# Dealing a top-p search out differently between TensorE's steps: first attention of a four-layer graph network

## The chip, the cores and the metric

The kernel runs on one core of a Trainium2 chip. The metric is the device time of one execution in microseconds (us), lower is better. Three executions of the kernel before took 3474.58, 3479.55 and 3481.09 us; their median is 3479.55 us.

## What is computed

There are 3327 nodes with 256 features each, and a dense adjacency of 3327 x 3327. Four layers follow one another, each of the form `x = layernorm(x + layer(x, adj))`. The change lies in layer 3:

```python
def _top_p_attention(X, W1, W2, W3):
    q = X @ W1.T @ W2.T
    k = X @ W3.T
    probs = softmax(q @ k.T / TAU, axis=-1)
    # keep the largest entries of each row until their sum reaches 0.9
    A = probs * mask
    return A / maximum(A.sum(-1, keepdims=True), 1e-12)

R = S + eye(N);  R = R / R.sum(-1, keepdims=True)
for n in range(2):
    A = _top_p_attention(Xa, W1, W2, W3)
    Xf = R @ Xf
    Xa = A @ Xa
    Z = Z + Xf @ U1[n].T + Xa @ U2[n].T
return layernorm(X + Z)
```

Here `S` is the adjacency. The loop over `n` runs twice; the change touches the first round only, "the first attention". For each row it needs scores against all nodes, a search for the value down to which entries are kept, the product of the kept entries with `X` (values), and the product of the adjacency's rows with `X` (the spread).

## The kernel before

Rows are worked in 26 tiles of 128, in 13 pairs (`nh`). A pair's two products, spread and values, are each made with a scheme that multiplies 2 x 2 blocks with seven products instead of eight. One step of such a product handles one of 13 column blocks with `products`: seven products, which the trace shows as fourteen matmul records. Before its products a spread step may need sums of adjacency blocks (`cb`, VectorE, in `part` of `diffused_pair`, one for two steps), and a value step needs sums of transposed weights (`sw`, VectorE, in `mix` of `attended_pair`). When 13 steps are done, `assembled` puts the seven partial results together into `c` with eight VectorE operations, which read the accumulator in PSUM. For the spread, `with_own` then adds each node's own part into `F`.

For the values, TensorE first transposes the weights: `turn` writes four transposed blocks into `tp` (two buffers), ScalarE copies them to `wt`, and VectorE mixes them to `sw` (three buffers). `attended_pair` makes three turns and two mixes when it is first advanced; after that each value step makes a turn three blocks ahead, a mix two blocks ahead and its products.

Scores of a tile (`scores`) come in four groups: each is two or more matmuls into the only `sc` buffer and a ScalarE copy into `e`. The search for a tile (`search_short`) is a generator in slices, and a call of `look` runs one slice of the search at the head of a queue: five slices of MAX8 over 26 segments (5, 5, 5, 5 and 6 of them), six rounds on the candidates (the first also starts ScalarE's exponential over the whole row), a crossing, which needs a short exponential on ScalarE and finds the smallest kept value, two slices that mask half a row each, and an end. `finish` runs what is left of the queue.

After the values of a pair, `first` projects each of its tiles in three more steps: transposes of the spread and value results into `tp` and a copy `xt`, a projection with a VectorE sum `s`, and the second projection with keys and queries for the next attention. Its beginning scales the values by a normalizer on ScalarE.

A pass of the main loop, for pair i, has two halves. The first half runs seven spread steps of pair i+1 (`stage`), four score groups of tile 2i+2, the projection of the preceding pair's even tile, and at step 5 `attend_to(i)`, which finishes the queue and starts the values of pair i. Then come value steps 0 to 6. The second half runs spread steps 7 to 12, the four score groups of tile 2i+3 and the projection of the odd tile, and then value steps 7 to 12. Between all these stand the looks. Ahead of the loop, tile 1's spread (`diffused_first`) and the scores of tiles 0 and 1 are made; behind it, the last two tiles.

The order on TensorE and VectorE is written out by hand in this stage: the wrappers `tensor` and `vector` keep every instruction of these two engines in program order (the trace puts them all on line 891, inside the wrapper, so they are told apart by their tiles). Instructions of ScalarE, GpSimd and the DMA queue on SP are put in order by the framework's planner. [...]

Of the kernel before, what the change touches and what calls it, by code (L numbers as in the profile page):

```python
# [50 lines left out]
def gnn_kernel(ctx: ExitStack, tc: tile.TileContext, n: int, a: dict, out: bass.AP):  # L51
# [3 lines left out]
    nh = nt // 2  # L55
# [121 lines left out]
    with tc.tile_pool(name="l1b", bufs=1) as wpool, tc.tile_pool(name="l1at", bufs=2) as l1at:  # L177
# [3 lines left out]
        with tc.tile_pool(name="l0", bufs=1) as pool, tc.tile_pool(name="l0w", bufs=2) as work, \  # L181
# [11 lines left out]
            for j0 in range(0, nh, J0):  # L193
                m = min(J0, nh - j0)
# [10 lines left out]
                y = slice(j0, j0 + m)  # L205
# [6 lines left out]
            for i in range(nh):  # L212
                p1, p2, p3, p4, p5, p6, p7 = halved(atp, cmb, psum, i, top, low, ts)
                c = work.tile([P, 2, D + 1], F32, name="c", bufs=1)
# [10 lines left out]
                for r in range(2):  # L225
                    it = 2 * i + r
# [3 lines left out]
                    y = work.tile([P, 2, HD], F32, name="y")  # L230
# [9 lines left out]
        with tc.tile_pool(name="l1aw", bufs=1) as cwork, tc.tile_pool(name="l1c", bufs=2) as ch, \  # L240
# [51 lines left out]
            for k, v in enumerate(("attn_src", "attn_dst")):  # L292
                r = scratch()[:, 0, :D]
# [17 lines left out]
            ends = []  # L311
# [219 lines left out]
            class Head:  # L531
# [70 lines left out]
                def finish(self):  # L602

                    c, w, e1 = self.c, self.w, self.e1
                    vec.tensor_sub(e1, e1, self.e)
                    vec.scalar_tensor_tensor(e1, self.v, 0.0, e1, op0=ALU.max, op1=ALU.add)
                    du = ch.tile([P, NG, WC], F32, name="du", bufs=1)[:, :, :w]
                    vec.tensor_mul(du, e1, us[c])
                    xs[c] = e1, du
# [103 lines left out]
            first = Head(0)  # L713
# [26 lines left out]
            turned = []  # L740
            for k, (c, s) in enumerate(states):
                w = us[c].shape[2]
                m = tiles_of(c)
# [59 lines left out]
                if c and 9 <= s < 9 + tiles_of(c - 1):  # L803
                    rs, nb = plus[:2]
                    i = s - 9
                    x = X[:, starts[c - 1] // P + i, :]
# [7 lines left out]
                if after:  # L814
                    if s == min(p["project"]):
                        pump(ends[c + 1] // P)
                    first = [lambda g=g: ahead.project(g) for g in p["project"].get(s, ())]
# [26 lines left out]
            m = tiles_of(nch - 1)  # L844
# [5 lines left out]
            for i in range(m):  # L850
                it = starts[nch - 1] // P + i
# [16 lines left out]
    with tc.tile_pool(name="l3", bufs=1) as pool, tc.tile_pool(name="l3d", bufs=1, space=DRAM) as dram:  # L868
# [135 lines left out]
        with tc.tile_pool(name="l2c", bufs=1) as cpool:  # L1004
# [5 lines left out]
            with tc.tile_pool(name="l2a", bufs=1) as wpool, \  # L1010
# [5 lines left out]
                r = cpool.tile([P, npad], F32, name="r")  # L1016
# [22 lines left out]
                m = wpool.tile([P, 2], F32, name="m")  # L1039
# [9 lines left out]
                f = wpool.tile([1, 1], F32, name="f")  # L1049
# [84 lines left out]
        tots, vs, kepts = ([pool.tile([P, nt], F32, name=f"{x}{p}") for p in range(2)] for x in ("tot", "v", "kept"))  # L1134
# [75 lines left out]
        def diffused_first(quads, psum, it, out):  # L1210

            own_part(it)
            acc = psum.tile([P, 2, 512], F32, name="acc")[:, 0, :D]
            for j0 in range(0, nt, 4 * JQ):
                m = min(4 * JQ, nt - j0)
                at = quads.tile([P, 5, JQ, P], F32, name="at", bufs=3).rearrange("p k j r -> p (k j) r")
                nc.sync.dma_start(at[:, :m, :], a["adjT"][it][:, j0:j0 + m, :])
                for j in range(m):
                    tensor.matmul(acc, at[:, j, :], X[:, j0 + j, :], start=(j0 + j == 0), stop=(j0 + j == nt - 1))
                yield  # L1220
            with_own(acc, it, out)

        def diffused_pair(quads, psum, i, b, out):
# [319 lines left out]
        def normalizer(sm, kept, total):  # L1543

            f = t1(sm, "f")
            vector.scalar_tensor_tensor(f, total, 1e-12, kept, op0=ALU.mult, op1=ALU.max)
            vector.reciprocal(f, f)
            return f
# [89 lines left out]
        with tc.tile_pool(name="l3w", bufs=2) as work, tc.tile_pool(name="l3s", bufs=4) as sm:  # L1638
# [13 lines left out]
            with tc.tile_pool(name="l3p", bufs=2, space=PSUM) as psum, tc.tile_pool(name="l3a", bufs=1) as quads:  # L1652
                fixed = True
                es, searches, xfs, todo, queue = {}, {}, [xf0], [], []
                flat = G.rearrange("p t d -> p (t d)")
                b = blocks(X, [flat[:, k * nh * HD:(k + 1) * nh * HD].rearrange("p (t d) -> p t d", t=nh) for k in range(4)])

                def look():
                    while queue and next(queue[0], queue) is queue:
                        queue.pop(0)  # L1660

                def finish():
                    while queue:
                        look()

                def logits(t):
                    return start(0, t, es, searches, search_short) if t < nt else iter(())

                def spreading(i):
                    x = diffused_pair(quads, psum, i, b, xfs) if i < nh else iter(())  # L1670
                    next(x, None)
                    return x

                def stage(spread, steps, groups, ends, then=lambda: None):
                    for k in range(steps):
                        next(spread, None)
                        if k % 2 == 0:
                            next(groups, None)
                        if k in (2, 3, 4):
                            next(ends, None)  # L1680
                        if k == 5:
                            then()
                        look()
                    for _ in groups:
                        pass
                    for _ in ends:
                        pass

                def attend_to(i):
                    turned[0] = attended_pair(quads, psum, (es[2 * i], es[2 * i + 1]), b)  # L1690
                    finish()
                    next(turned[0])

                turned = [None]
                for _ in logits(0):
                    pass
                queue.append(searches[0])
                spread = spreading(1)
                groups = logits(1)
                for _ in diffused_first(quads, psum, 1, xfs):  # L1700
                    next(groups, None)
                    for _ in range(3):
                        look()
                for _ in groups:
                    pass
                finish()
                queue.append(searches[1])
                for _ in range(7):
                    look()
                for i in range(nh - 1):  # L1710
                    ends = todo or [iter(()), iter(())]
                    stage(spread, 7, logits(2 * i + 2), ends[0], lambda: attend_to(i))
                    values = turned[0]
                    queue.append(searches[2 * i + 2])
                    for _ in range(7):
                        next(values)
                        look()
                    stage(spread, 6, logits(2 * i + 3), ends[1])
                    for _ in spread:
                        pass  # L1720
                    finish()
                    queue.append(searches[2 * i + 3])
                    for k in range(6):
                        if k == 3:
                            spread = spreading(i + 2)
                        next(values)
                        look()
                        if k % 3 == 2:
                            look()
                    c = next(values)  # L1730
                    todo = []
                    for r in range(2):
                        it = 2 * i + r
                        f = normalizer(sm, kepts[0][:, it:it + 1], tots[0][:, it:it + 1])
                        todo.append(first(quads, psum, it, c[:, r, :], f, xfs[it], "tp", c[:, r, :]))
                        next(todo[r])
                values = attended(quads, psum, es[nt - 2], X, acc=psum.tile([P, 2, 512], F32, name="acc")[:, 0, :D])
                next(values)
                ends = (x for y in todo for x in y)
                for it in (nt - 2, nt - 1):  # L1740
                    for _ in range(7):
                        acc = next(values)
                        if it == nt - 2:
                            look()
                            look()
                        next(ends, None)
                    acc = next(values)
                    if it == nt - 2:
                        finish()
                        values = attended(quads, psum, es[nt - 1], X, acc=psum.tile([P, 2, 512], F32, name="acc")[:, 0, :D])  # L1750
                        next(values)
                    f = normalizer(sm, kepts[0][:, it:it + 1], tots[0][:, it:it + 1])
                    c = quads.tile([P, 2, D], F32, name="c", bufs=1)[:, 0, :] if it == nt - 2 else quads.tile([P, 4, P], F32, name="sw", bufs=3)[:, :2, :].rearrange("p a b -> p (a b)")
                    for _ in ends:
                        pass
                    ends = first(quads, psum, it, acc, f, xfs[it], "tp", c)
                    next(ends)
                both(ends)
                fl0 = unresolved(sm, psum, 0)
                fixed = False  # L1760
# [210 lines left out]
```

## Time and profile before

The profile shows one execution. Times are in us.

| what | value |
|---|---|
| median of three executions | 3479.55 |
| the profiled execution, its own time | 3479.06 |
| its span, first to last instruction | 3477.3 |
| TensorE matmul busy | 3155.6 (91%) |
| VectorE busy | 2743.7 (79%) |
| ScalarE busy | 1738.5 (50%) |
| first attention, about | 1697 to 2617 |
| distance from pass to pass in it | 69.05 |
| mean granted TensorE clock, whole span | 0.966 |

"Busy" adds up the time in which an engine has an instruction under way. TensorE overlaps its matmuls, and their ends are modelled, so the distance from one start to the next says more than a duration. In timelines a row merges instructions of one kind that follow each other: start, time to the end of the last, engine, line, operation, output<-inputs, shape, count, and in brackets the idle time before and what ended it. `acc<-X,at`, `acc<-G,at` and `acc<-G,cb` are spread steps, `acc<-X,wt`, `acc<-G,sw`, `acc<-X,sw` and `acc<-G,wt` value steps, `tp<-ident,e` turns, `sc<-kT,q` scores, `tp<-U,xt` projections.

### The profile page before, as it was taken

Reading aid. Unit: us, or ns where it says so; the run is one execution under the profiler, and the core shown is the slowest. Engines: PE = TensorE matmul, PEld = TensorE weight load, DVE = VectorE, ACT = ScalarE, POOL = GpSimd, SP = SyncE. Lnnn points to the kernel's source line nnn. Section 1 sums busy time; section 2 is a strip of 40 time slices with the busy share of each in tenths; the row PEclk is TensorE's granted clock in tenths of the full one; section 3 lists DMA queues with packets and bytes.
Section 4 is the critical chain, followed back from the end, with each engine's and each line's share of the span. In section 5 each row is a group of like instructions: output and inputs, shape, how many; then the busy total and the mean of one; then the engine's idle time right before and its main releaser. Section 6 shows DMA issues by size and latency. Waiting matters only on the chain. (4 is left out here: it accounts for less than half of the span.)

```text
span 3477.3 us, 50356 instructions
## 1 busy us (share of the span) xinstructions
PE 3155.6 (91%) x18301; PEld 2570.0 (74%) x18301; DVE 2743.7 (79%) x6359; ACT 1738.5 (50%) x2764; POOL 938.9 (27%) x942
## 2 busy tenths in 40 slices
PE   8999888898987777999899999999998999999996
PEld 5998757676665555888678888888885777777775
DVE  4665368999999997777577777777755999999996
ACT  1000456766767774111233333333336888888883
POOL 0000245666656652111400000000002333333332
PEclk9999999999999988999999999999998999999998
DMA  6775334434343222444322322222213122222220
GB/s 198 253 246 183 114 90 127 109 106 121 101 114 87 68 60 97 147 143 153 97 74 62 88 66 80 63 87 67 79 40 105 56 63 70 62 68 66 66 66 16
DMA packets 206266, 344.32 MB, mean 99 GB/s; under 512 B 22223, under 2 KB 129167, under 8 KB 205871
## 3 DMA queue, kind: packets, MB, share of 16 engines
q1 hardware_dynamic: 205998, 340.92, 32.4%
q8 instruction: 148, 2.42, 0.3%
q14 instruction: 120, 0.98, 0.1%
HBM read 304.65 MB, written 36.21 MB: 98 GB/s over the span
## 5 line engine op out<-in xcount | busy, mean ns | idle before, releaser
L330 POOL TENSOR_TENSOR h<-du,row 128x2048 f32<-128x2048 f32 (+1 forms) x110 | 465.6, 4233 | 343.0 <-DVE hc L330 254.6
L330 DVE TENSOR_TENSOR_SCAN h<-dA,carry,h 128x512 f32<-128x512 f32 (+1 forms) x384 | 448.8, 1220 | 16.6 <-ACT dA L337 16.5
L337 ACT ACTIVATE dA<-t,A_log 128x512 f32<-128x512 f32 (+1 forms) x448 | 292.6, 658 | 147.2 <-DVE h L330 145.6
L1295 PE MATMUL acc<-F,at 128*128 128x256 f32 x1352 | 353.1, 387 | 0.0
L1340 PE MATMUL acc<-G,wt 128*128 128x256 f32 x1352 | 335.3, 391 | 5.7 <-ACT wt L1139 5.3
L389 PE MATMUL cb<-F,at 128*128 128x256 f32 x1196 | 296.3, 396 | 8.1 <-ACT hn L409 3.4
L1079 PE MATMUL acc<-F,at 128*128 128x257 f32 x1352 | 302.1, 380 | 1.3 <-ACT r L1023 1.3
L1340 PEld LDWEIGHTS acc<-G,wt 128*128 128x128 f32 x1352 | 249.4, 192 | 65.1 <-ACT wt L1139 35.1
L1295 PEld LDWEIGHTS acc<-F,at 128*128 128x128 f32 x1352 | 239.3, 191 | 72.4 <-issue 46.6
L680 PE MATMUL y<-ident,hc 128*128 128x128 f32 x1664 | 238.2, 298 | 46.4 <-DVE hc L330 46.1
L1079 PEld LDWEIGHTS acc<-F,at 128*128 128x128 f32 x1352 | 252.5, 190 | 36.5 <-issue 1.5
L680 PEld LDWEIGHTS y<-ident,hc 128*128 128x128 f32 x1664 | 212.4, 155 | 86.8 <-DVE hc L330 61.9
L389 PEld LDWEIGHTS cb<-F,at 128*128 128x128 f32 x1196 | 230.6, 199 | 58.7 <-issue 19.4
L1146 POOL MEMSET e<- 128x1 f32 x52 | 4.9, 98 | 934.0 <-PE tp L891 815.6
L330 DVE TENSOR_TENSOR hc<-h,row 128x2048 f32<-128x2048 f32 (+2 forms) x114 | 243.6, 2138 | 11.3 <-PE y L680 4.3
L891 PE MATMUL acc<-X,at 128*128 128x128 f32 (+1 forms) x988 | 174.9, 289 | 0.4 <-DMA at<-in_adjT 0.4
L891 PE MATMUL acc<-G,sw 128*128 128x128 f32 x936 | 157.2, 277 | 14.5 <-DVE sw L891 14.5
L138 PE MATMUL acc<-t,cb 128*128 128x128 f32 (+1 forms) x1014 | 168.4, 275 | 0.0
L891 PEld LDWEIGHTS acc<-X,at 128*128 128x128 f32 x988 | 144.0, 195 | 25.0 <-issue 21.9
L1262 ACT COPY wt<-tp 128x512 f32<-128x512 f32 x156 | 90.4, 587 | 132.8 <-PE tp L891 116.6
L891 PE MATMUL acc<-G,cb 128*128 128x128 f32 x624 | 122.6, 278 | 23.6 <-DVE cb L891 23.6
L1403 ACT ACTIVATE e<-e,neg 128x3328 f32<-128x3328 f32 x26 | 79.8, 3070 | 127.6 <-DVE neg L891 119.6
(417 smaller groups left out, 7154.8 us busy)
## 6 DMA issues: line engine op xcount, KB each, us to landing
at<-in_adjT SPq DMA_DIRECT2D x54, 832.0 KB, 4.5
at<-in_adjT SPq DMA_DIRECT2D x130, 320.0 KB, 3.0
row<-bc SPq DMA_DIRECT2D x80, 512.0 KB, 4.9
at<-in_adjT SPq DMA_DIRECT2D x52, 640.0 KB, 5.5
at<-in_adjT SPq DMA_DIRECT2D x52, 576.0 KB, 3.9
at<-in_adjT SPq DMA_DIRECT2D x72, 256.0 KB, 3.1
at<-mixed SPq DMA_DIRECT2D x72, 256.0 KB, 3.6
mixed<-cb SPq DMA_DIRECT2D x26, 640.0 KB, 4.1
```

Of the source, the lines that this page charges most:

```text
L138: mm = nc.tensor.matmul(acc, w[:, j, :], x, start=(y == 0 and k % 3 == 0 and k < 6), stop=(y == nh - 1 and k in (2, 6)))
L330: return lambda *x, **k: tc.keep_in_program_order(op(*x, **k))
L337: decays.append(op(*x, **k))
L389: ten.matmul(acc, at[:, j % JC, :], X0[:, j, :], start=(j == 0), stop=(j == nt - 1))
L680: x = ten.matmul(y[:, g * P:(g + 1) * P], h[:, g, i * P:(i + 1) * P], ident, is_transpose=True, start=(first and g == 0), stop=(last and g ...
L891: return lambda *x, **k: tc.keep_in_program_order(op(*x, **k))
L1079: nc.tensor.matmul(acc, at[:, j, :], F[:, j0 + j, :], start=(j0 + j == 0), stop=(j0 + j == nt - 1))
L1146: nc.gpsimd.memset(e[:, n:], NEG)
L1262: nc.scalar.copy(wts[-1], pt)
L1295: nc.tensor.matmul(acc, at[:, j, :], rhs[:, j0 + j, :], start=(j0 + j == 0), stop=(j0 + j == nt - 1))
L1340: tensor.matmul(acc, wt[:, j, :], rhs[:, j0 + j, :], start=(j0 + j == 0), stop=(j0 + j == nt - 1))
L1403: nc.scalar.activation(e, e, AF.Exp, bias=neg, accum_out=total)
```

## The change

The work itself stays; its order in the instruction streams changes. Looks get counts for each step, the end of a pair's values (assembly, normalizers, scaling) moves behind step 0 of the next first half, so that the sum `cb` that step 0 asks for (it serves steps 2 and 3) is issued ahead of it; the end of the spread (assembly and own part) moves behind value step 7; and the first searches run on into the first pass without a `finish`. Of a search begun in the second half, four slices instead of eight are run there.

```diff
@@ diffused_first
                     tensor.matmul(acc, at[:, j, :], X[:, j0 + j, :], start=(j0 + j == 0), stop=(j0 + j == nt - 1))
-                yield
+                    if j % 4 == 3 or j == m - 1:
+                        yield
@@
+                def looks(k):
+                    for _ in range(k):
+                        look()
+
-                def stage(spread, steps, groups, ends, then=lambda: None):
+                def stage(spread, steps, groups, ends, counts, then):
                     for k in range(steps):
                         next(spread, None)
+                        then.get(k, int)()
                         if k % 2 == 0:
                             next(groups, None)
                         if k in (2, 3, 4):
-                            next(ends, None)
-                        if k == 5:
-                            then()
-                        look()
+                            next(ends[0], None)
+                        looks(counts[k])
...
+                def end_pair(i):
+                    c = next(turned[0])
+                    for r in range(2):
+                        it = 2 * i + r
+                        f = normalizer(sm, kepts[0][:, it:it + 1], tots[0][:, it:it + 1])
+                        todo[r] = [first(quads, psum, it, c[:, r, :], f, xfs[it], "tp", c[:, r, :])]
+                        next(todo[r][0])
+                    ends[0] = todo[0][0]
+
+                groups = logits(0)
+                x = diffused_first(quads, psum, 1, xfs)
+                for _ in groups:
+                    next(x)
                 queue.append(searches[0])
                 spread = spreading(1)
                 groups = logits(1)
-                for _ in diffused_first(quads, psum, 1, xfs):
+                for _ in x:
                     next(groups, None)
-                    for _ in range(3):
-                        look()
+                    looks(2)
                 for _ in groups:
                     pass
-                finish()
                 queue.append(searches[1])
-                for _ in range(7):
-                    look()
+                counts = 7 * [4]
+                ends = [iter(())]
                 for i in range(nh - 1):
-                    ends = todo or [iter(()), iter(())]
-                    stage(spread, 7, logits(2 * i + 2), ends[0], lambda: attend_to(i))
+                    stage(spread, 7, logits(2 * i + 2), ends, counts,
+                          {0: lambda: end_pair(i - 1) if i else None, 5: lambda: attend_to(i)})
+                    counts = [1, 2, 2, 2, 2, 0, 0]
+                    queue.append(searches[2 * i + 2])
                     values = turned[0]
-                    queue.append(searches[2 * i + 2])
-                    for _ in range(7):
+                    for k in range(7):
                         next(values)
-                        look()
-                    stage(spread, 6, logits(2 * i + 3), ends[1])
-                    for _ in spread:
-                        pass
+                        looks(k in (1, 2, 4, 5, 6))
+                    stage(spread, 6, logits(2 * i + 3), todo[1], [2, 1, 2, 1, 2, 1], {})
                     finish()
                     queue.append(searches[2 * i + 3])
                     for k in range(6):
+                        next(values)
+                        if k == 0:
+                            for _ in spread:
+                                pass
                         if k == 3:
                             spread = spreading(i + 2)
-                        next(values)
-                        look()
-                        if k % 3 == 2:
-                            look()
-                    c = next(values)
-                    todo = []
-                    for r in range(2):
-                        it = 2 * i + r
-                        f = normalizer(sm, kepts[0][:, it:it + 1], tots[0][:, it:it + 1])
-                        todo.append(first(quads, psum, it, c[:, r, :], f, xfs[it], "tp", c[:, r, :]))
-                        next(todo[r])
+                        looks(k > 1)
+                end_pair(nh - 2)
+                todo = [x for y in todo for x in y]
```

More of the change, by code (lines that the diff above doesn't have):

```diff
@@ L1679, in stage @@
                         if k in (2, 3, 4):
-                            next(ends, None)
-                        if k == 5:
-                            then()
-                        look()
+                            next(ends[0], None)
+                        looks(counts[k])
                     for _ in groups:
                         pass
-                    for _ in ends:
+                    for _ in ends[0]:
                         pass
@@ L1694, in gnn_kernel @@
                 turned = [None]
-                for _ in logits(0):
-                    pass
+                none = [iter(())]
+                todo = [none, none]
+                def end_pair(i):
[10 more added lines that the diff above has]
+                    next(x)
                 queue.append(searches[0])
@@ L1699, in gnn_kernel @@
                 groups = logits(1)
-                for _ in diffused_first(quads, psum, 1, xfs):
+                for _ in x:
                     next(groups, None)
-                    for _ in range(3):
-                        look()
+                    looks(2)
                 for _ in groups:
                     pass
-                finish()
                 queue.append(searches[1])
-                for _ in range(7):
-                    look()
+                counts = 7 * [4]
+                ends = [iter(())]
                 for i in range(nh - 1):
-                    ends = todo or [iter(()), iter(())]
-                    stage(spread, 7, logits(2 * i + 2), ends[0], lambda: attend_to(i))
+                    stage(spread, 7, logits(2 * i + 2), ends, counts,
+                          {0: lambda: end_pair(i - 1) if i else None, 5: lambda: attend_to(i)})
+                    counts = [1, 2, 2, 2, 2, 0, 0]
+                    queue.append(searches[2 * i + 2])
                     values = turned[0]
-                    queue.append(searches[2 * i + 2])
-                    for _ in range(7):
+                    for k in range(7):
                         next(values)
-                        look()
-                    stage(spread, 6, logits(2 * i + 3), ends[1])
-                    for _ in spread:
-                        pass
+                        looks(k in (1, 2, 4, 5, 6))
+                    stage(spread, 6, logits(2 * i + 3), todo[1], [2, 1, 2, 1, 2, 1], {})
                     finish()
```

## The prediction

> **What bounds the kernel now.** I first read the page's busy shares, then a table by stretches of the first attention (about 1697 to 2617 us), then that stage's waits of TensorE, then the timelines of TensorE and VectorE through one pass. Starts of the assembly (VectorE's copy `c<-acc`) lie 69.05 us apart from pass to pass almost throughout, so one pass stands for all. One whole pass (columns: stretch, its length, busy us and instructions of PE, PEld, DVE, ACT, POOL, clock, DMA share, GB/s):
> ```profile
> 2157.00:2226.00 69.00, 65.38 (x498) 57.41 (x497) 51.96 (x177) 24.16 (x39) 0.20 (x2) 1.00 0.26 74
> ```
> TensorE is the bound, VectorE has 17 us to spare, and DMA is light. So only TensorE's holes can be won. In one pass its waits are (total, times, longest):
> ```profile
> PE acc L891 <- DVE sw L891: 1.6, 3, 1.3
> PE acc L891 <- DVE cb L891: 1.5, 1, 1.5
> PE tp L891 <- ACT wt L1262: 0.2, 1, 0.2
> ```
> VectorE has room but comes late. TensorE in the second half of a pass and at the start of the next (start, duration, instruction):
> ```profile
> 2157.81 2.76 PE L891 MATMUL tp<-U,xt 128*128 128x256 f32 x12
> 2165.93 1.04 PE L891 MATMUL tp<-ident,e 128*128 128x128 f32 x8
> 2167.21 0.66 PE L891 MATMUL tp<-ident,e 128*128 128x128 f32 x4 [0.24 <-ACT wt L1262]
> ...
> 2202.26 0.66 PE L891 MATMUL tp<-ident,e 128*128 128x128 f32 x4
> ...
> 2214.56 0.49 PE L891 MATMUL acc<-G,sw 128*128 128x128 f32 x2 [1.26 <-DVE sw L891]
> ...
> 2216.21 0.61 PE L891 MATMUL acc<-X,at 128*128 128x128 f32 x4
> ...
> 2220.43 0.61 PE L891 MATMUL acc<-X,at 128*128 128x128 f32 x4
> 2222.59 0.49 PE L891 MATMUL acc<-G,cb 128*128 128x128 f32 x2 [1.55 <-DVE cb L891]
> ```
> and what VectorE did meanwhile:
> ```profile
> 2160.60 0.42 DVE L891 TENSOR_TENSOR s<-tp,X 128x256 f32<-128x256 f32 x1 [3.18 <-PE tp L891]
> ...
> 2164.18 1.95 DVE L891 SCALAR_TENSOR_TENSOR e<-e,v 128x1664 f32<-128x1664 f32 x1
> ...
> 2211.56 2.03 DVE L891 MAX8 cand<-e 128x8 f32<-128x128 f32 x10
> 2213.50 0.67 DVE L891 TENSOR_TENSOR cb<-at 128x512 f32<-128x512 f32 x1
> 2214.09 0.42 DVE L891 TENSOR_TENSOR sw<-wt 128x256 f32<-128x256 f32 x1
> ...
> 2218.96 0.28 DVE L891 COPY c<-acc 128x128 f32<-128x128 f32 x1
> 2221.84 0.69 DVE L891 TENSOR_TENSOR cb<-at 128x512 f32<-128x512 f32 x1
> ```
> Two search slices (ten MAX8) stand ahead of a mix `sw` that TensorE waits for; the assembly of `c` stands ahead of the sum `cb`.
>
> [...] behind the idle 6.21 us that ends at 1742.43 a group of four score matmuls lasted 1.76 us, and 0.97 us in the steady passes, whose clock is 1.00. [...] each MAX8 is listed at 277 ns and five take 1.06 us, so I use distances between starts.
>
> **What is removed, pass by pass.** From rows: one spread step (seven products, fourteen records) is 1.56 us (2156.25 to 2157.81), a value step with a turn 2.00 (2172.31 to 2174.31), a score group 1.0.
> - Value steps 7 to 12 run from 2202.26 to 2216.21, 13.95 us; without waits 3 x 2.00 + 3 x 1.56 = 10.68. Hole: 3.28.
> - Spread step y=2: its first four matmuls start at 2220.43 and take 0.44, the next starts at 2222.59. Hole 1.72, with a slow restart 1.8.
> - Turn: eight transposes (0.88) from 2165.93, the next at 2167.21. Hole 0.4.
> Together 5.5, so a pass without holes is 63.6 us.
>
> **What VectorE does afterwards.** Starts to starts: mix 0.98, five MAX8 1.01, six 1.17, search round 0.88 (the last 0.37), crossing 0.76, a half of the mask 1.88, `cb` 0.61 to 0.65, assembly 2.33, two normalizers 0.55, own part 0.79, `xt` 0.61, `s` 0.35.
> Second half, t=0 at spread step 7: TensorE reaches the projection `tp<-U,xt` of the odd tile at 8.8, its end at 11.4; value steps run 17.95 to 28.6. VectorE is idle before `xt` (3 us) and before `s`; from 11.6: s, last round, crossing (its exponential on ScalarE 0.4 after the round), both mask halves: ends 17.4. Then mix 9, assembly and own part to 21.5, mix 10 to 22.5 (needed 23.95), mix 11 to 23.5 (needed 25.5), slice, mix 12 at 25.5 (needed 27.06), `cb`, three slices: ends 29.2. All mixes are early, so the 3.28 goes.
> Next pass, t=0 at step 0: `cb` for step 2 at 0.6 to 1.25 (needed 4.7), so the 1.8 goes. Assembly to 3.6, normalizers 4.1, six MAX8 5.3, two rounds 7.1, `cb` 7.7, `xt` 8.3; the projection wants it at 8.8: just in time. Scaling on ScalarE (0.9) is done by 5, its transposes start at 6.8.
> Now the new lateness. `s` waits for the projection (before: 2160.60 - 2157.81 = 2.79 behind its start), so VectorE resumes at 8.83 + 2.79 = 11.62 with four more things than before ahead of the mask: two rounds 1.25, crossing, first half. s 0.35, rounds 1.25, `cb` 0.61, crossing 0.79, mask 1.87 + 1.95: ends 18.45. TensorE's turns come 8.12 behind the projection's start, at 16.95; only the fourth transpose reads the second half of the odd tile (before, turns started at 2165.93, ahead of the mask's end at 2166.1), so it waits from 17.28 to 18.5. New hole 1.3 with restart; the next turn then waits for `wt`'s copy 0.45. Behind that transpose on TensorE stand the other turns, spread step 6, the fourth score group and the value steps; VectorE's first two mixes wait for it, and nothing that TensorE needs earlier. Net per pass: 5.5 - 1.75 = 3.75.
>
> **Moved at no cost.** DMA orders are as before: `at` loads are released by the same products (a load issued at 2220.40 follows step 1), 3.2 us to landing, and are wanted 9 us later. On SP nothing is queued behind a new wait: the stores of `s` follow the same steps. ScalarE's 3.07 us exponential moves to the start of a half (done at 4.3, the next score copy is needed at 5.9) and to 6.2-9.4, where the next score group comes at 13; if that cover went, up to 3 us per pass.
>
> **Ends of the stage.** Beginning: VectorE now sits 8.21 us before the own part (1730.49). Afterwards the own part waits less, but logits 0 wait for an adjacency load, slices start some 4 us later, and `cb` waits for a load; I get the second tile's mask at about 1751.7 instead of 1754.2, but TensorE has done its work by 1740 and starts half clocked, about 2.5 lost. I take -1 (range -6 to +4). End: the last assembly no longer stands behind 2.6 us of search (the transposes of `c` at 2566.85 waited 2.49 us and a half-clock window of 3.4 us followed, 1.7 lost); some comes back as the exponential delays turns: +2.
>
> **Sum.** The holes of the first pass's second half 3.3; 11 full passes x 3.75 = 41.2; the last pass's holes were 0.7 smaller: -0.7; ends -1 + 2. Total 44.8 (24 to 55). I round to 43, since every term but the beginning was read at its most favourable. The profiled execution took 3479.06 (span 3477.3 and 1.8 around it), the median is 3479.55: 3436.5.
>
> **Rivals.**
> - *ScalarE orders the exponential of the tops behind a score copy* (its order is a planner's; margin 0.85 us, since the tops are ready at 13.25 and that group ends at 14.0). For: two rounds later than now. Against: in the second half today the same pair stood right, by 1.7 us. Then crossing starts 1.45 later, 11 x 1.45 = 16: 3452.
> - *The turn doesn't stall*, if a round or `s` is quicker than read: 11 x 1.75 = 19 more: 3418.
> - *Slower*: in the first half the 3.07 us exponential of the odd tile's scores is put behind the third score copy, ending at 18.2. Then limit, crossing and mask end at 22.9; the turn waits 5.7 instead of 1.3[...]. Hole 7.9 against 5.5: 11 x 2.4 = 26 lost, less 5 won at the first and last pass: 3500. It decides once the turn's wait exceeds 1.3 + 3.75 = 5.0 us. Against: scores' tops are ready 7 us ahead of that copy.
> - *It does nothing*: another engine paces the pass. Against: VectorE 52 of 69, ScalarE 24; holes are named.
>
> **Chances.** Forecast 0.64; score copy ahead 0.20; no stall 0.05; slower 0.07; nothing 0.04. Faster 0.89, same 0.04, slower 0.07; 0.2% (7 us) is about what a measurement here can tell. Eight in ten: 3426 (a good beginning, smaller stall) to 3457 (score copy ahead).
>
> **What would show it.** Distance of assemblies 65.3 us instead of 69.05; no waits for `sw` in value steps 7 to 12, none for `cb` in step 2; a new wait of TensorE `tp` on VectorE `e`, 1.2 us, once a pass; crossing's exponential ahead of the third score copy. Wrong if that wait is over 2 us, if `xt` is late, or if the beginning loses more than 6 us.

## The result and the profile after

| | before | changed |
|---|---|---|
| median of 4 executions each | 3477.95 | 3429.9 |
| lowest to highest | 3474.58 to 3481.09 | 3424.49 to 3433.41 |
| the profiled execution | 3479.06 | 3429.23 |
| its span | 3477.3 | 3427.4 |

The ratio is 0.9861, with a 95% interval of 0.9844 to 0.9878: faster by 48 us, where 43 were forecast (3436.5 us; measured 3429.9).

One pass of the first attention, in the table by stretches of the changed kernel (the same columns as before):

```profile
2180.00:2245.30 65.30, 64.00 (x499) 56.96 (x498) 52.13 (x177) 24.29 (x40) 0.20 (x2) 1.00 0.27 78
```

VectorE and ScalarE are busy as long as before (51.96 and 24.16 us then); the pass is 65.30 us instead of 69.05. What TensorE still waits for in one pass, in its list of waits:

```profile
PE tp L891 <- DVE e L891: 1.1, 1, 1.1
PE tp L891 <- ACT wt L1263: 0.2, 1, 0.2
```

The waits for `sw` and `cb` are gone, and a wait of the turns for the mask of the odd tile (`e`) is new. TensorE's timeline in that pass shows both:

```profile
2192.10 0.61 PE L891 MATMUL acc<-X,at 128*128 128x128 f32 x4
2192.55 0.39 PE L891 MATMUL acc<-G,cb 128*128 128x128 f32 x2
...
2196.72 2.76 PE L891 MATMUL tp<-U,xt 128*128 128x256 f32 x12
...
2204.84 0.49 PE L891 MATMUL tp<-ident,e 128*128 128x128 f32 x3
2206.39 0.77 PE L891 MATMUL tp<-ident,e 128*128 128x128 f32 x5 [1.06 <-DVE e L891]
2207.39 0.66 PE L891 MATMUL tp<-ident,e 128*128 128x128 f32 x4 [0.24 <-ACT wt L1263]
```

Step 2 runs straight on (0.45 us from the start of its first four matmuls, which the row lists with 0.61, to the next; 2.16 before). Three transposes of the first turn go, the fourth waits. VectorE's timeline says why:

```profile
2188.26 0.67 DVE L891 TENSOR_TENSOR cb<-at 128x512 f32<-128x512 f32 x1
2188.85 0.28 DVE L891 COPY c<-acc 128x128 f32<-128x128 f32 x1
...
2199.51 0.43 DVE L891 TENSOR_TENSOR s<-tp,X 128x256 f32<-128x256 f32 x1 [1.83 <-PE tp L891]
...
2204.38 1.95 DVE L891 SCALAR_TENSOR_TENSOR e<-e,v 128x1664 f32<-128x1664 f32 x1
```

VectorE sits idle 1.83 us before `s`, and from there to the mask's end at 2206.3 it works without a gap. ScalarE's order, on which a rival rested, came out as forecast: its timeline has the exponential of the tops ahead of the third score copy.

```profile
2201.14 0.33 ACT L1408 ACTIVATE top<-top,neg 128x48 f32<-128x48 f32 x1 [0.80 <-DVE top L891]
2201.98 0.85 ACT L1160 COPY e<-sc 128x832 f32<-128x832 f32 x1 [0.51 <-PE sc L891]
```

Two smaller edits of the second half show too. In the kernel before, VectorE waited for TensorE and then ended the spread between the two halves of the mask, so that the mixes came behind both (from 2206.66 on):

```profile
2201.47 0.29 DVE L891 COPY c<-acc 128x128 f32<-128x128 f32 x1 [1.62 <-PE acc L891]
...
2204.60 1.95 DVE L891 SCALAR_TENSOR_TENSOR e<-e,v 128x1664 f32<-128x1664 f32 x1
```

In the changed kernel the mask ends first, a mix follows, and the end of the spread comes only then:

```profile
2176.70 0.42 DVE L891 TENSOR_TENSOR sw<-wt 128x256 f32<-128x256 f32 x1
...
2177.69 0.28 DVE L891 COPY c<-acc 128x128 f32<-128x128 f32 x1
```

And the mix that value step 10 makes now stands ahead of the next pair's first `cb` (0.6 us), which stood ahead of it before (2213.50 and 2214.09 in the prediction's rows).

**Where the 49.8 us between the two profiled executions went.** I cut the stage at points that TensorE reaches in both kernels:

| stretch | before | after | gain |
|---|---|---|---|
| first score group to value step 0 of the first pass | 61.41 | 62.29 | -0.88 |
| value step 0 of the first to that of the last pass (11 passes) | 757.14 | 714.05 | 43.09 |
| of it one pass that held 3.41 us at half clock before | 71.01 | 65.31 | 5.70 |
| last pass, value steps 0 to 12 | 41.95 | 40.69 | 1.26 |
| value step 12 to the stage's last small matmul | 55.50 | 50.14 | 5.36 |
| all outside the stage | 2561.26 | 2560.27 | 0.99 |

At the beginning of the stage VectorE still waits for tile 1's spread (first row, VectorE's timeline), and TensorE then waits for the second mask (the other two, TensorE's timeline):

```profile
1725.04 0.48 DVE L891 SCALAR_TENSOR_TENSOR F<-acc,rdeg,F 128x256 f32<-128x256 f32 x1 [5.79 <-PE acc L891]
```

```profile
1749.87 0.45 PE L891 MATMUL tp<-ident,e 128*128 128x128 f32 x1 [8.98 <-DVE e L891]
1751.65 0.69 PE L891 MATMUL tp<-ident,e 128*128 128x128 f32 x2 [1.33 <-DVE e L891]
```

At its end the transposes of the last pair's `c` no longer wait 2.49 us; they follow 0.34 us behind those of the spread (TensorE's timeline):

```profile
2517.55 0.38 PE L891 MATMUL tp<-ident,F 128*128 128x128 f32 x2
2517.89 0.44 PE L891 MATMUL tp<-ident,c 128*128 128x128 f32 x2
```

### The profile page after: what moved, and what is told of

The parts are those of the page before. It is cut to its first block, busy times and chain, and to the rows that moved or that the text cites. A ratio compares the mean times of both kernels' runs of the same rounds, so it can differ in the third digit from the quotient of the medians.

```text
span 3427.4 us, 50359 instructions
## 1 busy us (share of the span) xinstructions
PE 3141.9 (92%) x18301; PEld 2566.4 (75%) x18301; DVE 2745.2 (80%) x6359; ACT 1738.6 (51%) x2764; POOL 937.4 (27%) x942
## 5 line engine op out<-in xcount | busy, mean ns | idle before, releaser
L891 DVE MAX8 cand<-e 128x8 f32<-128x128 f32 x676 | 139.8, 277 | 5.4 <-ACT e L1160 3.6
L1160 ACT COPY e<-sc 128x832 f32<-128x832 f32 x78 | 65.9, 845 | 149.5 <-PE sc L891 149.5
```

The source lines that it names most:

```text
L891: return lambda *x, **k: tc.keep_in_program_order(op(*x, **k))
```

## The experiments

Two questions stood open. The kernel got faster by two things in the main loop, the sum ahead of the assembly and the new dealing of the search (with which I count the later end of the spread and the later `cb`): which of them did it? And is the wait that is left really set by what VectorE has behind `s`? All runs do the whole computation. Distances of passes are from the profiles; times outside this stage differ by up to 6.5 us between profiles (2558.5 to 2565.0), so the distances are the finer measure. Each ratio is to executions of the kernel before made alongside that run (medians 3479.0 and 3479.9), with its 95% interval in brackets.

### The sum ahead of the assembly, alone

In the kernel before, with `at0` standing for `end_pair(i - 1)` of the change:

```diff
                         next(spread, None)
+                        if k == 0:
+                            at0()
...
-                    c = next(values)
-                    todo = []
-                    for r in range(2):
...
```

> The kernel before, with one part of the change alone: the end of a pair's values (assembly, normalizers, scaling) stands behind spread step 0 of the next pass, so that the sum cb for step 2 is ahead of it; the search is dealt out as before. Theory (every hole of TensorE is VectorE's lateness, and both parts treat the same lateness): the 1.8 us hole before step 2 goes, the 3.3 us in value steps 7 to 12 stay, and xt comes about 0.5 us late for the projection: 11 x 1.3 = 14 us less than before, about 3464. Rival (the sum's place does most of the work): about 3440, and the holes in the value steps shrink too.

Measured 3463.76 us, ratio 0.9965 (0.9951 to 0.9979). Passes are 67.67 us apart, 1.37 less than 69.04, where 1.3 was expected. The waits of one pass, in its list:

```profile
PE acc L891 <- DVE sw L891: 1.6, 3, 1.3
PE tp L891 <- ACT wt L1262: 0.2, 1, 0.2
PE tp L891 <- DVE xt L891: 0.2, 1, 0.2
```

The wait for `cb` is gone, those for `sw` stand untouched, and one of 0.2 us for `xt` has come: TensorE, no longer held up at step 2, now reaches the projection before VectorE, as late as before, has made `xt`.

### The dealing, without the sum's move

In the changed kernel:

```diff
-                          {0: lambda: end_pair(i - 1) if i else None, 5: lambda: attend_to(i)})
+                          {5: lambda: attend_to(i)})
...
                         looks(k > 1)
-                end_pair(nh - 2)
+                    end_pair(i)
```

> The changed kernel with one part undone: the end of a pair's values again at the end of the pass, ahead of the sum cb for step 2; the dealing of the search, the later end of the spread and the beginning stay as changed. Theory: with the new dealing VectorE is at the assembly when TensorE has just finished, 0.6 us into step 0; assembly 2.3, normalizers 0.6 and cb 0.6 end at 4.1, and step 2 wants cb at 4.7: no hole, the same time as the changed kernel, 3430 within 2. Rival (the place of the sum matters by itself): the hole of 1.8 us is back in 11 passes, 3450.

Measured 3429.79 us, ratio 0.9863 (0.9845 to 0.9881), passes 65.30 us apart: the changed kernel's numbers. VectorE's timeline shows that the assembly at 2187.05 is followed by the sum,

```profile
2187.05 0.27 DVE L891 COPY c<-acc 128x128 f32<-128x128 f32 x1
...
2189.93 0.69 DVE L891 TENSOR_TENSOR cb<-at 128x512 f32<-128x512 f32 x1
```

which ends at 2190.6, while TensorE's timeline has step 2 begin at 2190.90 and take its `cb` products without a gap:

```profile
2190.90 0.61 PE L891 MATMUL acc<-X,at 128*128 128x128 f32 x4
2191.35 0.39 PE L891 MATMUL acc<-G,cb 128*128 128x128 f32 x2
```

So the sum's place isn't needed: with the dealing it gains nothing that was measured. The first experiment's 1.37 us per pass and these 3.75 do not add up, since both cure the same lateness.

This run keeps the later end of the spread and the later `cb` along with the new numbers of looks, and neither was tried alone. They may matter: in the kernel before VectorE sat idle 1.62 us at that end of the spread. With the second half of the mask put into that idle time, all the mixes behind it would come some 1.7 us sooner (an estimate from those rows, with the looks as before), about half of the 3.28 us that value steps 7 to 12 lost. How the gain divides between these edits and the looks stays open.

### Two search rounds ahead of `s`

```diff
-                    counts = [1, 2, 2, 2, 2, 0, 0]
+                    counts = [1, 2, 4, 0, 2, 0, 0]
```

> The changed kernel with two search rounds moved: looks 1, 2, 4, 0, 2, 0, 0 in the first half instead of 1, 2, 2, 2, 2, 0, 0, so that rounds 4 and 5 stand ahead of the projection's sum s, where VectorE is idle 1.8 us. Theory (the turn waits for the mask, whose end is s plus all that VectorE has behind it): the mask ends 1.25 us earlier, the wait of 1.06 us goes, 11 x 1.2 = 13 to 14 us less, about 3416, passes 64.1 us apart. Rival (the turn's wait has another setter, ScalarE's exponentials or a load): 3430, passes still 65.3 apart. Other rival (the rounds make s late): a new wait behind the projection, 3430 or more.

Measured 3418.3 us, ratio 0.983 (0.9813 to 0.9846), passes 64.14 us apart (64.1 expected). In VectorE's timeline its idle time before `s` fell from 1.83 to 0.53 us, and the mask's second half starts at 2196.18:

```profile
2192.47 0.42 DVE L891 TENSOR_TENSOR s<-tp,X 128x256 f32<-128x256 f32 x1 [0.53 <-PE tp L891]
...
2196.18 1.95 DVE L891 SCALAR_TENSOR_TENSOR e<-e,v 128x1664 f32<-128x1664 f32 x1
```

TensorE's turns, which come at 2197.80, go through all eight transposes; only the wait for ScalarE's copy is left in its timeline:

```profile
2197.80 1.15 PE L891 MATMUL tp<-ident,e 128*128 128x128 f32 x8
2199.19 0.66 PE L891 MATMUL tp<-ident,e 128*128 128x128 f32 x4 [0.24 <-ACT wt L1263]
```

### One search round more behind `s`

```diff
-                    counts = [1, 2, 2, 2, 2, 0, 0]
+                    counts = [1, 2, 1, 3, 2, 0, 0]
```

> The changed kernel with one search round more behind s: looks 1, 2, 1, 3, 2, 0, 0. Theory: the mask ends one round (0.88 us) later, and so does the turn: 11 x 0.88 = 10 us more, 3440, passes 66.2 apart, the wait of the turn 1.9 us. Rival (another setter): 3430, wait unchanged at 1.06.

Measured 3452.16 us, ratio 0.9929 (0.9912 to 0.9945): 22 us over the changed kernel, where 10 were expected. Two passes are 66.18 us apart, 0.88 more, as the theory says; eight are 67.6 to 67.8. The first, shorter pass too is 0.87 longer. In the list the wait of the fourth transpose is 1.54 us (1.9 expected, 1.06 in the changed kernel); by starts the turn loses 2.10 us instead of 1.22, which is the 0.88. In a longer pass the clock is at half behind the wait. The table by stretches over its turn and the time behind it (last columns: granted clock, DMA share, GB/s):

```profile
2215.70:2219.20 3.50, 1.54 (x11) 1.12 (x11) 2.59 (x7) 1.08 (x2) 0.00 (x0) 0.99 0.51 137
2219.20:2222.60 3.40, 3.40 (x18) 3.17 (x18) 3.01 (x9) 0.59 (x1) 0.00 (x0) 0.50 0.26 76
```

11 x 0.88 = 9.7 and 8 x 1.57 = 12.6, what the longer passes have over 66.18, make 22.3; the eleven passes took 736.27 us against 714.05, 22.2 more. So the end of the mask sets the wait: it moved with the number of rounds in both directions. The expectation left out the clock, 0.50 in the second stretch.

### The changed beginning, alone

In the kernel before, `diffused_first` and the lines ahead of the loop are those of the change, and the first pass has four looks a step.

> The kernel before with the changed beginning alone (first searches run on into the first pass, tile 1's spread in steps of four). The main loop is as before. Theory: VectorE comes to the first mask's end 2 to 3 us earlier, but TensorE has then long been idle and starts at half clock: from the first score group to value step 0 of the first pass 61 to 62.5 us (before 61.4, changed 62.3), the rest as before; a time within 3 us of the kernel before. Rival (the beginning carried part of the gain): 57 us or less.

One execution: 3475.99 us, beside a median of 3479.9 for the kernel before. From the first score group to value step 0 it took 60.29 us (before 61.41, changed 62.29), a little under the 61 to 62.5 expected; the passes are as before, 69.05, with one of 71.00. The same beginning took 60.89 to 62.29 in the profiles of the changed kernel and of the three runs that alter only its main loop, so differences of 1 to 2 us here can't be told apart. Of the gain of 48 us the new beginning carries nothing that shows.

### The third turn behind spread step 6

On the run with early rounds:

```diff
-            for j in range(3):
+            for j in range(2):
                 turn(j)
+            yield None
+            turn(2)
             for j in range(2):
                 mix()
...
-                          ... 5: lambda: attend_to(i)})
+                          ... 5: lambda: attend_to(i), 6: lambda: next(turned[0])})
```

> The run with rounds 4 and 5 ahead of s, and besides the third turn (with the first two mixes) behind spread step 6 instead of straight behind the second. Theory: the third turn no longer waits for ScalarE's copy of the first (0.24 us by the waits, 0.4 from start to start): 12 x 0.4 = 5 us less than that run, about 3413, passes 63.7 apart. Rival (the mixes come too late for value step 0): passes 64.1 or more.

Measured 3415.74 us, ratio 0.9817 (0.9802 to 0.9832), passes 63.68 us apart, as expected (63.7), and no wait of TensorE is left in a pass. Of 5 us in the eleven passes (701.26 to 696.23) the median shows 2.6, within the spread of the executions (3412.98 to 3418.67); in its profile the time outside the stage was 4 us longer than with early rounds alone.

### The own part of tile 1 later

In the changed kernel:

```diff
-                for _ in x:
+                for _ in range(3):
+                    next(x)
                     next(groups, None)
                     looks(2)
                 for _ in groups:
                     pass
+                looks(6)
...
-                          {0: lambda: end_pair(i - 1) if i else None, 5: ...
+                          {0: lambda: end_pair(i - 1) if i else next(x, None), 5: ...
```

> The changed kernel with VectorE's own part for tile 1 moved from ahead of search rounds 1 to 5 and the crossing to behind spread step 0 of the first pass, so that VectorE does not sit idle 5.8 us for TensorE's last matmuls of that spread. Theory (VectorE paces the beginning): the first pair's mask ends 4.7 us earlier, from the first score group to value step 0 57.6 us instead of 62.3, up to 2.4 less if TensorE's clock no longer halves; 3423 to 3425. Rival (TensorE or the loads pace the beginning): unchanged, 3430.

Measured 3424.17 us, ratio 0.9845 (0.983 to 0.986); from the first score group to value step 0 56.47 us instead of 62.29. The stall before the own part is gone from VectorE's timeline; a shorter one, for a load, stands ahead of it:

```profile
1722.55 0.69 DVE L891 TENSOR_TENSOR cb<-at 128x512 f32<-128x512 f32 x1 [1.37 <-DMA at<-mixed]
1723.16 0.48 DVE L891 SCALAR_TENSOR_TENSOR F<-acc,rdeg,F 128x256 f32<-128x256 f32 x1
```

VectorE paced the beginning: TensorE's wait for the second mask fell from 8.98 us to 1.00. The gain was 5.8 us where 4.7 to 7 were expected.

### All three

> Rounds 4 and 5 ahead of s, the third turn behind spread step 6, and the own part behind spread step 0 of the first pass, all on the changed kernel. Theory (the three holes are apart from each other, so gains add up): 14 + 5 + 6 less than the changed kernel, about 3406. Rival (one hole covers another): 3413 or more.

Measured 3406.16 us (3399.17 to 3412.78), ratio 0.9788 (0.9769 to 0.9807). Passes are 63.68 us apart, the beginning took 53.23 us. The table by stretches over one pass:

```profile
2100.00:2163.68 63.68, 63.68 (x498) 56.95 (x498) 52.41 (x176) 24.16 (x39) 0.20 (x2) 1.00 0.27 80
```

TensorE is busy for the whole of it, and 63.6 us was the prediction's sum for a pass without holes. The gains added up: in the eleven passes 17.8 us, which are the 12.8 of the early rounds and the 5.0 of the third turn. The beginning gained 9.1 us, 3.2 more than with the own part alone. Most of this is the clock: from the turns' last wait for the mask to value step 0 it took 4.1 us instead of 7.0. TensorE's timelines list the first four spread matmuls behind the turns with 0.61 us here (at 1748.22) and 1.06 there (at 1745.16), the length that they have in the changed kernel at 1753.71, where the granted clock is 0.50. This version beats both kernels, with a median 24 us under the changed one.

## Why the prediction was right

The direction, the range and the main mechanism held: VectorE's lateness made the holes, an earlier VectorE closed them, and a smaller wait for the mask came in their place. One attribution was wrong, and one term of the sum was only half of what it measured. Point by point:

- **Holes removed.** 3.28 us in value steps 7 to 12, 1.8 before step 2: both gone. The 1.8 has a slow restart of 0.1 in it: the start behind the wait, at 2222.59, is 0.32 us ahead of the next, 0.22 without a wait (2220.21 to 2220.43). The pass was forecast at 65.3 us apart and measured 65.30.
- **The new hole.** Forecast: the fourth transpose waits 1.2 us, 1.3 with the restart, then 0.45 for `wt`. Measured: 1.06 idle, then 0.24 idle; starts show 1.22 and 0.44 lost. Two experiments moved it down by 1.16 us and up by 0.88.
- **Which part removes the 1.8.** The step "`cb` for step 2 at 0.6 to 1.25 (needed 4.7), so the 1.8 goes" gave it to the sum's place. That was wrong as an attribution: without the sum's move it ends 0.3 us before step 2 begins, so the 1.8 goes all the same. The total was not touched by it.
- **Just in time.** `xt` at 8.3 for a projection at 8.8: no wait showed. With the sum's move alone, where VectorE is later, it waits 0.2 us.
- **The beginning.** -1 was forecast, -0.88 measured. The reason was the one given: counted from the first score group the second mask ends 1.0 us earlier (1751.60 instead of 1754.22 in its profile, but the stage began 1.6 us earlier there), and TensorE, idle for 8.98 and 1.33 us before it, takes 1.9 us more from there to value step 0, with a granted clock of 0.50 from 1746.26 to 1756.50. That the figure fits so well is luck, since the same beginning took 60.89 to 62.29 us in four profiles.
- **The end.** +2 was forecast. The last pair of rows in the table of stretches gained 6.62 us together; 2.6 of it was counted as the last pass's hole, so the end gave 4.0. This is the term that was mis-sized: I let the exponential take back some of the wait of 2.49 us and the 1.7 lost to the clock, and the transposes of `c` now follow without either: the granted clock is 1.00 from 1756.50 to 2565.46, where it was 0.50 from 2566.77 to 2570.19 before. Up to 1.6 us of the 4.0 need not be the change's: the run with the changed beginning alone, which ends like the kernel before, took that much less there.
- **Half clock in one pass.** In the kernel before one pass took 71.01 us, 1.97 more than the others, and had a granted clock of 0.50 from 1877.28 to 1880.69; the sum left that out. In the changed kernel the clock is 1.00 through these passes.
- **The rounding.** The sum was 44.8, and I took 43 "since every term but the beginning was read at its most favourable". The stage gave 48.8 in the profiles: 44.8, 2.0 from the end, 2.0 from that pass. The discount pointed the wrong way.

Of the rivals, the one on ScalarE's order did not occur: the exponential stood 0.84 us ahead of the score copy, with 0.85 foreseen (the prediction's own times, 13.25 and 14.0, are 0.75 apart). The slower rival, an exponential behind the third copy, did not occur either. Its hole of 7.9 us is the wait of 5.7, 0.45 for `wt` and 1.7 for half clock, my estimate from the 1.7 that the kernel before lost behind a wait of 2.49 us. Something like it did follow a shorter wait: in the run with one round more the turn lost 2.10 us, and eight of the ten full passes lost another 1.57. So the 5.0 us at which the gain was to be used up, which left the clock out, is too high; with 1.57 more in each pass it would be some 3.4 (an estimate from these numbers).

## What to carry to other kernels

When a nearly full engine waits for one that has room, ask where in its order the room lies: moving two rounds of search into an idle stretch of 1.8 us was worth some 12 us, though no work was saved. If several edits cure the same lateness, try each alone: here one that the prediction credited, the sum's place, added nothing to the others. Look too at what stands behind a wait for the other engine: one round more behind `s` made the turn lose 0.88 us more, two rounds put ahead of it made the pass 1.16 us shorter. So put as much as fits ahead of such a wait.

## What the hardware showed unexpectedly

Waits of TensorE of 1.5 to 2.5 us were followed by half clock in some places and not in others. In the kernel before, the wait for `cb` in step 2 was 1.55 us in the pass of the prediction's rows, with a clock of 1.00, and 1.90 us in the pass of 71.01 us (TensorE's timeline, the first of the two rows below, which stands ahead of 3.41 us at 0.50). At the end of its stage 3.41 us at 0.50 stood behind 2.49 us for `c`.

```profile
1875.76 0.49 PE L891 MATMUL acc<-G,cb 128*128 128x128 f32 x2 [1.90 <-DVE cb L891]
...
1877.08 1.60 PE L891 MATMUL sc<-kT,q 64*128 64x416 f32 x4
```

The four score matmuls of the second row are listed with 1.60 us, and with 0.97 where the clock is 1.00 (at 2128.35). In the changed kernel the turn lost 1.22 us in each of the eleven passes, and the clock stayed at 1.00 from 1756.50 to 2565.46, so it cost only itself. With one round more the turn lost 2.10 us (waits of 0.17 and 1.54); the table shows 0.50 in the 3.40 us behind one such turn, and eight of the ten full passes lost another 1.57. What decides whether half clock follows was not shown.
